# Norm of queries and keys on VectorE, middle butterfly on GpSimd, and issue order planned by phase

## The chip, the cores and the metric

One core of a Trainium2 chip. The metric is the device time of one launch in microseconds, median of the runs. One execution is also profiled; its trace gives the single durations. Engines are named as in the profile: PE (TensorE), PEld (its weight loads), DVE (VectorE), ACT (ScalarE), POOL (GpSimd), SP (SyncE, which issues the DMAs).

## What is computed

The input x is 128 x 32 x 256 (batch B, steps T, features N). Layer 0 integrates a coupled neuron model over the 32 steps (a fourth-order Runge-Kutta step per t) and sends each state through a feed-forward block with block-scaled quantization; the sum with x is the input of layer 1. Layer 1, on which the change lies, is an attention with normed queries and keys, 16 heads of 16, over the 32 tokens of each batch row, and then a feed-forward block with Hadamard rotation and ternary weights:

```
qkv = xn @ W_qkv
q = rms_norm(q, g_q);  k = rms_norm(k, g_k)          # over the 16 features of a head, eps 1e-6
attn = softmax(q k^T * 16 ** -0.5);  o = attn @ v
f = o + o @ W_out
gate, up = h_bitlinear(f, w_gate), h_bitlinear(f, w_up)
x = x + h_bitlinear(silu(gate) * up, w_down)

h_bitlinear(x, w) = act_quant(fwht(x)) @ weight_quant(w).T   # fwht: Walsh-Hadamard transform
```

## The kernel before

The kernel writes down all of its work as a list of items (`Work.add`): engine, a cost in us, a function that issues the instructions, the buffers read and written, and a rank. A buffer (`Buf`) is one of several slots of a pool (`wide`, `mid`, `slim`, `tiny` in SBUF; `ps_one`, four slots of one PSUM bank each, and `ps_two`, two slots of two banks, in the second phase). A planner then orders the list (`Work.order`, `Work.run`). `run` is a list scheduler over the five engines with costs, gaps between engines (`TAIL`, `HOP`, `WITHIN`), a shared port of DVE and POOL (`port=True`), slots that come free, and activation tables; run backward it gives priorities. `order` alternates the two 40 times and keeps the order with the earliest end, over both phases together. `emit` issues the items in that order, first all with a rank under 100 (phase one), then the rest (phase two). Engines take their instructions in the order of issue. `keep_warm` puts multiplications by zeros into long planned gaps of PE.

`fills=` adds an item to the writers of a buffer, so that later readers wait for it, but lets the item itself wait for nobody who wrote or read that buffer before.

Phase one (to about 430 us in the trace) has 32 steps: `step` (the integration, lines L552 to L653) and `ffn0` (layer 0's feed-forward block, L895 to L1017), and prepares the weights. Its last items per step write `xnT`, the normed and turned input of layer 1.

Phase two is `tokens(g)` for 32 groups g of 128 tokens each. Several groups are under way at a time. Per group:

- L1125, L1132: PE multiplies for queries and keys (`pqk`, 128 x 512) and for values (`pv`, columns 0 to 255 of a `ps_one` bank). L1141: ACT copies the values into `v_pad`. L1142: ACT squares `pqk` into `sq`.
- The norm: L1143, a DVE reduce over the 16 features of a head, gives 32 sums per token (`tiny`, 128 x 32). Function `rsqrt` (L1084 to L1111): POOL scales them (L1088), DVE makes a first estimate of the inverse root with integer arithmetic on the bits (L1091), and POOL improves it in ten operations (L1099 to L1109).
- L1148 and L1155: DVE multiplies queries and keys in `pqk` by it, into `qn` and `k_pad`; `pqk` is free then. L1160: POOL multiplies the queries by the gains `g_prod`, which also carry the constant `RSQRT**-2`.
- L1167, L1169: DVE transposes. L1177: logits on PE (32 x 32 tiles). L1192, L1196: DVE maximum and difference; L1199: ACT exponential; L1200: DVE transpose; L1207: PE, attention times values. L1218, L1221: DVE reciprocal and product. L526: PE transposes (a helper's line). L1230: PE, output and rotation.
- Quantization (L1071 reduce, L1078, L1079 scales; L1240; ACT L1246, L1250), a transposing DMA, L1263: gate and up, L1271: ACT silu, L1278: DVE product, into `it` (128 x 1024).
- The butterflies (L1294): three stages of the rotation, two additions of 128 x 512 each (sum and difference). In groups 0 to 28 the stages run on POOL, DVE, POOL; in 29 to 31 all on DVE.
- L526 turn, L1300 ACT copy, L1305 PE rotation by a 128 x 128 Hadamard matrix, quantization (L1071, L1310, L1313, L1317), a transposing DMA, L1328 down-projection, L1335 DVE sum, store.

L666, L671 and L678, small DVE operations of phase one in `mx_scales`, have an operand in PSUM.

Of the kernel before, what the change touches and what calls it, by code (L numbers as in the profile page):

```python
# [13 lines left out]
I32 = mybir.dt.int32  # L14
AF = mybir.ActivationFunctionType
ALU = mybir.AluOpType
AX = mybir.AxisListType
# [16 lines left out]
HEADS = 16  # L34
D_HEAD = 16
EPS_RMS = 1e-6
EPS_QUANT = 1e-5
RSQRT = 8.0 / 3.0

# [60 lines left out]
class Work:  # L100
# [81 lines left out]

    def run(self, forth):

# [9 lines left out]
        port, table = 0.0, None  # L194
        self.issued, self.last, self.gone = [], dict.fromkeys(ready), set()
        for item in self.items:
            item.open = len(item.after if forth else item.before)
            item.ready = 0.0
            for b in item.bufs:
                b.left, b.end = 0, 0.0  # L200
                if b.slots and not b.fixed:
                    b.slot = None
                for s in b.slots:
                    s.free = 0.0
        pools = {}
        for item in sorted(self.items, key=lambda i: i.prio):
            for b in item.bufs:
                if b.slots and b.slot is None and not b.left:
                    b.pool = pools.setdefault(id(b.slots), [])
                    b.pool.append(b)  # L210
                b.left += 1
        for item in self.items:
            if not item.open:
                ready[item.engine].append(item)
        done = []
        while len(done) < len(self.items):
            best = None
            for e, waiting in ready.items():
# [13 lines left out]
                if best is None or (t, item.prio) < (best[0], best[1].prio):  # L232
                    best = (t, item)
            assert best is not None, "every item waits for a slot"
            t, item = best
            ready[item.engine].remove(item)
            idle = item.engine == PE and t > now[PE] + 0.05
            item.start, item.end = t, t + item.cost + (self.COLD if idle else 0.0)
# [19 lines left out]
            for i in item.before if forth else item.after:  # L258
                i.ready = max(i.ready, item.end + (self.gap(item, i) if forth else self.gap(i, item)))
                i.open -= 1  # L260
                if not i.open:
                    ready[i.engine].append(i)
        return done

    def order(self):

        for item in self.items:
            for a in item.after:
                a.before.append(item)
            for b in item.bufs:  # L270
                b.fixed = b.slot is not None
            item.prio = item.rank
        best = math.inf
        for n in range(self.ROUNDS):
            self.strict = n > 0
            done = self.run(True)
            end = max(item.end for item in done)
            if end < best:
                best, chosen = end, done
                places = [(b, b.slot) for item in done for b in item.bufs]  # L280
                times = [(item, item.start, item.end) for item in done]
                ends = [(b, b.end) for item in done for b in item.bufs]
            for item in self.items:
                item.prio = -item.end
            self.strict = True
            self.run(False)
            for item in self.items:
                item.prio = -item.end
        for b, slot in places:
            b.slot = slot  # L290
        for b, end in ends:
            b.end = end
        for item, start, end in times:
            item.start, item.end = start, end
        self.keep_warm(chosen)
        return chosen
# [26 lines left out]
def kernel(  # L323
# [570 lines left out]
    def ffn0(t, q):  # L894
# [100 lines left out]

        add(POOL, 0.72, rsqrt, [], [ms], rank=rank)
        if t < T - LATE:
# [51 lines left out]
    for b_c, c_mat in zip(b_coup[:KPADS], coup):  # L1049
        k_pad = c_mat.rearrange("p c n -> p (c n)").rearrange("p (r a d) -> p r a d", a=4, d=D_HEAD)  # L1050
        pads_ready.append(
            add(POOL, 0.6, lambda k_pad=k_pad: nc.gpsimd.memset(k_pad, 0.0), [], [b_c], rank=float(T))
        )
        k_pads.append(Slot(k_pad))
# [8 lines left out]
    def heads(ap):  # L1063
        return ap.rearrange("p (h d) -> p h d", d=D_HEAD)
# [18 lines left out]

    def rsqrt(v, y, scale, eps, rank):  # L1084

        t, u = Buf(tiny), Buf(tiny)
        tt, ts = nc.gpsimd.tensor_tensor, nc.gpsimd.tensor_scalar
        add(POOL, 0.24, lambda: ts(v.ap, v.ap, scale, eps, MULT, ADD), [], [v], rank=rank)  # L1088
        add(
            DVE, 0.12,  # L1090
            lambda: nc.vector.tensor_scalar(  # L1091
                y.ap.bitcast(I32), v.ap.bitcast(I32), -0.5, float(0x5F3759DF), MULT, ADD
            ),
            [v], [y], rank=rank,
        )

        def steps():

            tt(t.ap, y.ap, y.ap, MULT)  # L1099
            tt(t.ap, t.ap, v.ap, MULT)  # L1100
            ts(t.ap, t.ap, -0.5, 1.5, MULT, ADD)
            tt(y.ap, y.ap, t.ap, MULT)

            tt(t.ap, y.ap, y.ap, MULT)
            tt(t.ap, t.ap, v.ap, MULT)
            ts(u.ap, t.ap, 1.0, -10.0 / 3.0, MULT, ADD)
            tt(u.ap, u.ap, t.ap, MULT)
            ts(u.ap, u.ap, 1.0, 5.0, MULT, ADD)
            tt(y.ap, y.ap, u.ap, MULT)  # L1109

        add(POOL, 2.4, steps, [v], [t, u, y], rank=rank, port=True)  # L1111

    def tokens(g):
# [25 lines left out]
        v_pad, sq, qn, k_pad = Buf(v_pads), Buf(mid), Buf(slim), Buf(k_pads)  # L1139
        sq_sum, rstd = Buf(tiny), Buf(tiny)  # L1140
        add(ACT, 0.26, lambda: nc.scalar.copy(v_pad.ap[:, :, :D_HEAD], heads(pv.ap[:, :N])), [pv], [v_pad], rank=rank)  # L1141
        add(ACT, 0.477, lambda: nc.scalar.activation(sq.ap, pqk.ap, AF.Square), [pqk], [sq], rank=rank)  # L1142
        add(DVE, 0.6, lambda: nc.vector.tensor_reduce(sq_sum.ap, heads(sq.ap), AX.X, ADD), [sq], [sq_sum], rank=rank)  # L1143

        rsqrt(sq_sum, rstd, 1.0 / D_HEAD, EPS_RMS, rank)
        add(
# [37 lines left out]
        for k in range(0, PAIRS, PAIRS // 2):  # L1184
            add(
                PE, 0.55, lambda k=k: logits(range(k, k + PAIRS // 2)), [qT, kT], fills=[pl], rank=rank,
                records=BT * PAIRS, small=True,
            )
# [23 lines left out]
        for k in range(0, HEADS, HEADS // 2):  # L1212
            add(
                PE, 0.63, lambda k=k: attend(range(k, k + HEADS // 2)), [exT, v_pad], fills=[po], rank=rank,
                records=BT * HEADS, small=True,
            )
# [67 lines left out]
        src = it  # L1284
        for s, engine in enumerate((POOL, DVE, POOL) if g < NT - 3 else (DVE, DVE, DVE)):
            dst = Buf(wide)
            for e, op in enumerate((ADD, SUB)):
# [7 lines left out]

                add(engine, 0.6 if engine == DVE else 1.228, butterfly, [src], fills=[dst], rank=rank, port=True)
            src = dst
# [119 lines left out]
```

## Time and profile before

| | us |
|---|---|
| runs of the kernel before | 867.62, 867.91, 868.57 (median 867.91) |
| the profiled execution's own time | 868.0 |
| its span in the trace, first to last instruction | 866.2 |
| busy in the span: PE, DVE, POOL, ACT | 795.1, 732.2, 615.9, 494.0 |
| butterflies L1294 on POOL: 116 of 1306 ns | 149.1 in all |
| butterflies L1294 on DVE: 76 of 727 ns | 53.3 in all |
| norm on POOL, L1088 and L1099 to L1109, 352 operations | 89.2 in all |
| L1091 on DVE: 32 of 321 ns | 10.3 in all |

A busy share is an average over stages with different limits, so the tables of stretches of the trace and the lists of waits are to be read by stage. The end of a PE instruction is modelled, since matmuls are pipelined. In a list of waits, a line names the waiting engine, its output and line, then the releaser, then the total in us, how many times, and the longest. In a timeline a line gives start, duration, engine, line, operation, output and inputs, and in brackets how long the engine had been idle and who released it. Durations of neighbours on DVE overlap, so that what one instruction costs its engine is the distance from start to start.

### The profile page before, as it was taken

To read this page: it belongs to the slowest core of one execution; us is meant where nothing else is said; L and a number is where in the kernel's file an instruction comes from. 1 tells how busy PE (TensorE), PEld (TensorE's weight loads), DVE (VectorE), ACT (ScalarE), POOL (GpSimd) and SP (SyncE) were. 2 spreads that over 40 slices of the span, in tenths; PEclk is the share of its full clock that TensorE was granted. 3 is DMA by queue.
4 is the path that set the end of the run, shared out by engine and by line. 5 is a ranking of instruction groups with operands and counts; after the bars stand their busy time and mean duration, and the time that the engine had idled before them with its cause. 6 is when DMAs were issued, how large, how long until landed. Compare 5 with 4: busy or idle time off the path is not lost. (4 is left out here: it accounts for less than half of the span.)

```text
span 866.2 us, 26286 instructions
## 1 busy us (share of the span) xinstructions
PE 795.1 (92%) x10506; PEld 598.6 (69%) x10506; DVE 732.2 (85%) x1863; ACT 494.0 (57%) x1009; POOL 615.9 (71%) x955
## 2 busy tenths in 40 slices
PE   7789999999999999997789999999999999899986
PEld 4566778877788788775456667666667676576765
DVE  6889989999989999998677887778878788887694
ACT  3233465655466665754335667666767555776755
POOL 5698898888768888899574776656685676676320
PEclk9999999999999999999799999999999999999999
DMA  7222232313122242435500113221221221221334
GB/s 241 84 38 53 59 82 59 74 49 83 35 65 68 70 134 56 92 67 110 117 2 15 27 39 65 49 49 32 52 50 48 56 48 42 48 43 46 60 68 86
DMA packets 128891, 55.53 MB, mean 64 GB/s; under 512 B 102144, under 2 KB 127616, under 8 KB 128768
## 3 DMA queue, kind: packets, MB, share of 16 engines
q1 hardware_dynamic: 128768, 53.85, 26.9%
q8 instruction: 82, 1.34, 0.6%
q14 instruction: 41, 0.34, 0.1%
HBM read 21.32 MB, written 8.39 MB: 34 GB/s over the span
## 5 line engine op out<-in xcount | busy, mean ns | idle before, releaser
L1294 POOL TENSOR_TENSOR wide<-wide 128x512 f32<-128x512 f32 x116 | 149.1, 1306 | 68.7 <-DVE wide L1278 33.6
L601 PEld LDWEIGHTS ps_stage<-slim,coup 128*128 128x128 f32 x1024 | 129.3, 192 | 18.1 <-ACT slim L594 10.6
L601 PE MATMUL ps_stage<-slim,coup 128*128 128x128 f32 x1024 | 139.4, 279 | 0.6 <-ACT slim L594 0.3
L608 POOL TENSOR_TENSOR slim<-slim,slim 128x256 f32<-128x256 f32 x96 | 72.4, 755 | 27.7 <-ACT slim L595 23.0
L587 PE MATMUL ps_stage<-slim,eye 128*128 128x256 f32 x256 | 76.6, 392 | 8.1 <-DVE slim L552 7.8
L587 PE MATMUL ps_stage<-drives,eye 128*128 128x256 f32 x256 | 79.2, 392 | 3.3 <-DVE ps_stage L552 2.0
L956 POOL TENSOR_TENSOR mid<-mid,tiny 128x512 f32<-128x512 f32 x64 | 66.2, 1047 | 3.7 <-DVE tiny L678 3.2
L964 POOL TENSOR_TENSOR wide_bf<-mid,tiny 128x512 bf16<-128x512 fp8e4 x64 | 66.5, 1050 | 1.4 <-DVE mid L888 1.1
L594 ACT ACTIVATE slim<-slim 128x256 f32<-128x256 f32 x96 | 39.3, 409 | 47.4 <-DVE slim L552 44.6
L1305 PE MATMUL ps_two<-had_ffn,wide 128*128 128x128 f32 x512 | 63.3, 278 | 1.3 <-DVE wide L1278 1.2
L595 ACT ACTIVATE slim<-slim 128x256 f32<-128x256 f32 x96 | 39.2, 408 | 43.1 <-DVE slim L552 43.0
L1305 PEld LDWEIGHTS ps_two<-had_ffn,wide 128*128 128x128 f32 x512 | 59.9, 192 | 5.4 <-ACT wide L1300 1.9
L1125 PE MATMUL ps_one<-w_qkv_sb,xnT 128*128 128x512 f32 x128 | 60.7, 599 | 0.5 <-DVE mid L1196 0.2
L1313 ACT ACTIVATE wide<-ps_two,magic,tiny 128x1024 f32<-128x1024 f32 x32 | 38.5, 1203 | 39.5 <-DVE tiny L1079 28.0
L587 PEld LDWEIGHTS ps_stage<-slim,eye 128*128 128x128 f32 x256 | 42.0, 190 | 24.0 <-DVE slim L552 16.1
L1294 DVE TENSOR_TENSOR wide<-wide 128x512 f32<-128x512 f32 x76 | 53.3, 727 | 5.9 <-POOL wide L1294 5.9
L1278 DVE SCALAR_TENSOR_TENSOR wide<-ps_two,tiny,mid 128x512 f32<-128x512 f32 x64 | 46.4, 737 | 12.0 <-ACT mid L1271 11.3
L1207 PEld LDWEIGHTS ps_one<-v_pad,mid 32*32 32x32 f32 x4096 | 42.2, 106 | 20.8 <-issue 15.4
L1271 ACT ACTIVATE mid<-ps_two,tiny 128x512 f32<-128x512 f32 x64 | 43.0, 686 | 21.9 <-PE ps_two L1263 21.6
L1207 PE MATMUL ps_one<-v_pad,mid 32*32 32x17 f32 x4096 | 48.0, 181 | 4.5 <-issue 3.0
L587 PEld LDWEIGHTS ps_stage<-drives,eye 128*128 128x128 f32 x256 | 40.3, 193 | 12.3 <-DVE ps_stage L552 7.7
L1263 PEld LDWEIGHTS <-slim_bf 128*128 128x128 bf16 x256 | 24.0, 97 | 34.3 <-issue 8.3
(169 smaller groups left out, 2188.7 us busy)
## 6 DMA issues: line engine op xcount, KB each, us to landing
x_step<-in_x_dram SPq DMA_DIRECT2D x32, 128.0 KB, 2.1
x_add<-in_x_dram SPq DMA_DIRECT2D x32, 128.0 KB, 2.1
x_dram<-slim SPq DMA_DIRECT2D x32, 128.0 KB, 1.9
slim<-x_dram SPq DMA_DIRECT2D x32, 128.0 KB, 2.6
out_dram<-slim SPq DMA_DIRECT2D x32, 128.0 KB, 1.7
raws<-in_L_ffn_w_gate_dram SPq DMA_DIRECT2D x4, 512.0 KB, 4.8
raws<-in_L_ffn_w_up_dram SPq DMA_DIRECT2D x4, 512.0 KB, 6.3
raws<-in_L_ffn_w_down_dram SPq DMA_DIRECT2D x4, 512.0 KB, 4.0
```

Source lines behind the costliest of these rows:

```text
L587: PE, cost, lambda: nc.tensor.matmul(ps[i].ap, lhsT=eyes[eye], rhs=src.ap, start=False, stop=False),
L594: add(ACT, 0.32, lambda: nc.scalar.activation(th.ap, qi.ap, AF.Tanh), [qi], [th], rank=rank, table="silu")
L601: nc.tensor.matmul(ps[i].ap[:, sl], lhsT=coup[i][:, c, sl], rhs=two(th.ap)[:, c, :], start=False, stop=(c == NC - 1 and m == NC - 1),)
L608: POOL, 0.685, lambda: nc.gpsimd.tensor_tensor(sq.ap, sq.ap, qi.ap, MULT),
L956: lambda it=it, ks=ks: nc.gpsimd.tensor_tensor(blocks(it.ap), blocks(it.ap), spread(binv.ap[:, ks], BLOCK), MULT),
L964: lambda b8=b8, ks=ks, sl=sl: nc.gpsimd.tensor_tensor(blocks(bq.ap[:, sl]), blocks(b8.ap), spread(bscl.ap[:, ks], BLOCK), MULT),
L1125: nc.tensor.matmul(pqk.ap, lhsT=xnT_flat[:, c, tok], rhs=w_qkv_sb[:, c, : 2 * N], start=(c == 0), stop=(c == NC - 1),)
L1207: nc.tensor.matmul(by_v(po.ap)[row, hd, :], lhsT=by_head(exT.ap)[row, hd, :], rhs=v_pad.ap[row, hd, :], start=True, stop=True,)
L1271: lambda pgu=pgu, act=act: nc.scalar.activation(act.ap, pgu.ap[:, :HALF], AF.Silu, scale=sgu.ap[:, 0:1]),
L1278: lambda pgu=pgu, act=act, sl=sl: stt(it.ap[:, sl], pgu.ap[:, HALF:], sgu.ap[:, 1:2], act.ap, MULT, MULT),
L1294: eng.tensor_tensor(dv[:, :, e, :], sv[:, :, 0, :], sv[:, :, 1, :], op)
L1305: nc.tensor.matmul(pfh.ap[:, sl], lhsT=iT.ap[:, sl], rhs=had_ffn, start=True, stop=True)
```

## The change

Three things are changed.

The norm: the sum over a head is written into the bank of `pv`, beside the values (columns 256 to 351, three pieces of 32). From there nine DVE operations, in one item with the reduce, scale it, make the estimate from the bits, and correct it by a cubic polynomial in the estimate's error. Each has an operand in PSUM. All of `rsqrt` on POOL is gone. The constant `RSQRT` is that of the polynomial.

The butterflies: groups 0 to 26 run all three stages on POOL; groups 27 to 31 run DVE, DVE, POOL.

The planner: `order` plans the phases one after the other, the second from where the first leaves engines and slots, each with 40 rounds (and two passes of new priorities in a round); dependencies across phases set only the earliest start. Some costs differ, and PE's restart cost is booked from a gap of 0.15 us on (0.05 before).

```diff
-RSQRT = 8.0 / 3.0
+RSQRT = 3.64945348
...
-    def run(self, forth):
+    def run(self, items, forth, before):
...
+            for a in item.after if forth else item.before:
+                if a in self.gone:
+                    item.ready = max(item.ready, a.end + self.gap(a, item))
+                elif (a.rank < self.SECOND) == (item.rank < self.SECOND):
+                    item.open += 1
...
+        if forth:
+            for item in before:
+                now[item.engine] = max(now[item.engine], item.end)
...
-            idle = item.engine == PE and t > now[PE] + 0.05
+            idle = item.engine == PE and t > now[PE] + 1.5 * self.COLD
...
-        best = math.inf
-        for n in range(self.ROUNDS):
-            self.strict = n > 0
-            done = self.run(True)
...
+        for second in (False, True):
+            items = [item for item in self.items if (item.rank >= self.SECOND) == second]
+            best = math.inf
+            for n in range(self.ROUNDS):
+                self.strict = n > 0
+                done = self.run(items, True, chosen)
...
+                for back in (True, False):
+                    for item in items:
+                        item.prio = -item.end
+                    if back:
+                        self.strict = True
+                        self.run(items, False, ())
...
-        add(POOL, 0.72, rsqrt, [], [ms], rank=rank)
+        add(POOL, 0.86, rsqrt, [], [ms], rank=rank)
...
-            add(POOL, 0.6, lambda k_pad=k_pad: nc.gpsimd.memset(k_pad, 0.0), [], [b_c], rank=float(T))
+            add(POOL, 1.0, lambda k_pad=k_pad: nc.gpsimd.memset(k_pad, 0.0), [], [b_c], rank=float(T))
...
-    def rsqrt(v, y, scale, eps, rank):
...
+    POLY = (-1.14571778, 1.36854794, -1.82472059, RSQRT)
+
+    def norms(sq, y, place, scale, eps, rank):
...
+        n = 2 * HEADS
+        x, e, t = Buf(tiny), Buf(tiny), Buf(tiny)
+        ts = nc.vector.tensor_scalar
 
         def steps():
...
+            v, g, u = (place.ap[:, N + k * n : N + (k + 1) * n] for k in range(3))
+            nc.vector.tensor_reduce(v, heads(sq.ap), AX.X, ADD)
+            ts(x.ap, v, scale, eps, MULT, ADD)
+            ts(g.bitcast(I32), x.ap.bitcast(I32), -0.5, float(0x5F3759DF), MULT, ADD)
+            nc.vector.tensor_tensor(t.ap, g, x.ap, MULT)
+            nc.vector.tensor_tensor(u, g, t.ap, MULT)
+            ts(e.ap, u, -1.0, None, ADD)
+            stt(u, u, POLY[0] - 1.0, e.ap, ADD, MULT)
+            stt(u, u, POLY[1], e.ap, ADD, MULT)
+            stt(t.ap, u, POLY[2], e.ap, ADD, MULT)
+            stt(y.ap, t.ap, POLY[3], g, ADD, MULT)
+
+        add(DVE, 1.55, steps, [sq], [x, e, t, y], fills=[place], rank=rank)
...
-        add(DVE, 0.6, lambda: nc.vector.tensor_reduce(sq_sum.ap, heads(sq.ap), AX.X, ADD), [sq], [sq_sum], rank=rank)
-
-        rsqrt(sq_sum, rstd, 1.0 / D_HEAD, EPS_RMS, rank)
+        norms(sq, rstd, pv, 1.0 / D_HEAD, EPS_RMS, rank)
...
-                PE, 0.55, lambda k=k: logits(range(k, k + PAIRS // 2)), [qT, kT], fills=[pl], rank=rank,
+                PE, 0.48, lambda k=k: logits(range(k, k + PAIRS // 2)), [qT, kT], fills=[pl], rank=rank,
...
-                PE, 0.63, lambda k=k: attend(range(k, k + HEADS // 2)), [exT, v_pad], fills=[po], rank=rank,
+                PE, 0.57, lambda k=k: attend(range(k, k + HEADS // 2)), [exT, v_pad], fills=[po], rank=rank,
...
-        for s, engine in enumerate((POOL, DVE, POOL) if g < NT - 3 else (DVE, DVE, DVE)):
+        for s, engine in enumerate((POOL, POOL, POOL) if g < NT - 5 else (DVE, DVE, POOL)):
...
-                add(engine, 0.6 if engine == DVE else 1.228, butterfly, [src], fills=[dst], rank=rank, port=True)
+                add(engine, 0.6 if engine == DVE else 1.25, butterfly, [src], fills=[dst], rank=rank, port=True)
```

More of the change, by code (lines that the diff above doesn't have):

```diff
@@ L194, in run @@
         port, table = 0.0, None
-        self.issued, self.last, self.gone = [], dict.fromkeys(ready), set()
-        for item in self.items:
-            item.open = len(item.after if forth else item.before)
+        self.issued, self.last, self.gone = [], dict.fromkeys(ready), set(before)
+        for item in items:
+            item.open = 0
             item.ready = 0.0
+            for a in item.after if forth else item.before:
[3 more added lines that the diff above has]
+                    item.open += 1
             for b in item.bufs:
@@ L204, in run @@
                     s.free = 0.0
+        if forth:
+            for item in before:
+                now[item.engine] = max(now[item.engine], item.end)
+                self.last[item.engine] = item
+                table = item.table or table
+                for b in item.bufs:
+                    for s in b.slots:
+                        s.free = 0.0
+            for item in before:
+                for b in item.bufs:
+                    if b.slots:
+                        s = b.slots[b.slot]
+                        s.free = max(s.free, item.end + item.tail + self.TAIL[item.engine] + 0.06)
         pools = {}
-        for item in sorted(self.items, key=lambda i: i.prio):
+        for item in sorted(items, key=lambda i: i.prio):
             for b in item.bufs:
@@ L211, in run @@
                 b.left += 1
-        for item in self.items:
+        for item in items:
             if not item.open:
@@ L215, in run @@
         done = []
-        while len(done) < len(self.items):
+        while len(done) < len(items):
             best = None
@@ L258, in run @@
             for i in item.before if forth else item.after:
[L259 to L262, printed above, removed]
+                if (i.rank < self.SECOND) == (item.rank < self.SECOND):
+                    i.ready = max(i.ready, item.end + (self.gap(item, i) if forth else self.gap(i, item)))
+                    i.open -= 1
+                    if not i.open:
+                        ready[i.engine].append(i)
         return done
@@ L272, in order @@
             item.prio = item.rank
-        best = math.inf
-        for n in range(self.ROUNDS):
-            self.strict = n > 0
-            done = self.run(True)
[L277 to L294, printed above, removed]
+        chosen = []
+        for second in (False, True):
[4 more added lines that the diff above has]
+                done = self.run(items, True, chosen)
+                end = max(item.end for item in done)
+                if end < best:
+                    best, order = end, done
+                    places = [(b, b.slot, b.end) for item in done for b in item.bufs]
+                    times = [(item, item.start, item.end) for item in done]
+                for back in (True, False):
+                    for item in items:
+                        item.prio = -item.end
+                    if back:
+                        self.strict = True
+                        self.run(items, False, ())
+            for b, slot, end in places:
+                b.slot, b.end = slot, end
+            for item, start, end in times:
+                item.start, item.end = start, end
+            chosen += order
         self.keep_warm(chosen)
@@ L1082, in quantum @@
         return am, sc
-    def rsqrt(v, y, scale, eps, rank):
[L1086 to L1095, printed above, removed]
-        def steps():
[L1099 to L1111, printed above, removed]
+    POLY = (-1.14571778, 1.36854794, -1.82472059, RSQRT)
[3 more added lines that the diff above has]
+        ts = nc.vector.tensor_scalar
+        def steps():
+            v, g, u = (place.ap[:, N + k * n : N + (k + 1) * n] for k in range(3))
[10 more added lines that the diff above has]
+        add(DVE, 1.55, steps, [sq], [x, e, t, y], fills=[place], rank=rank)
     def tokens(g):
@@ L1139, in tokens @@
         v_pad, sq, qn, k_pad = Buf(v_pads), Buf(mid), Buf(slim), Buf(k_pads)
-        sq_sum, rstd = Buf(tiny), Buf(tiny)
+        rstd = Buf(tiny)
         add(ACT, 0.26, lambda: nc.scalar.copy(v_pad.ap[:, :, :D_HEAD], heads(pv.ap[:, :N])), [pv], [v_pad], rank=rank)
         add(ACT, 0.477, lambda: nc.scalar.activation(sq.ap, pqk.ap, AF.Square), [pqk], [sq], rank=rank)
-        add(DVE, 0.6, lambda: nc.vector.tensor_reduce(sq_sum.ap, heads(sq.ap), AX.X, ADD), [sq], [sq_sum], rank=rank)
-        rsqrt(sq_sum, rstd, 1.0 / D_HEAD, EPS_RMS, rank)
+        norms(sq, rstd, pv, 1.0 / D_HEAD, EPS_RMS, rank)
         add(
```

## The prediction

> **What bounds the kernel now.** I read the table of stretches first, because the change lies almost wholly in the second phase (from about 430 us). Columns: stretch, its length, busy us of PE (instructions), PEld, DVE, ACT, POOL, then granted clock, DMA share, GB/s.
>
> ```profile
> 430.00:440.00 10.00, 8.91 (x30) 4.85 (x31) 3.87 (x9) 3.12 (x6) 3.98 (x15) 1.00 0.14 27
> ...
> 600.00:650.00 50.00, 46.27 (x981) 34.53 (x981) 39.74 (x96) 34.28 (x48) 35.08 (x64) 0.97 0.22 49
> 650.00:700.00 50.00, 46.23 (x1045) 35.32 (x1044) 40.85 (x97) 31.03 (x45) 32.12 (x52) 1.00 0.20 48
> ...
> 820.00:840.00 20.00, 17.75 (x121) 12.34 (x120) 18.30 (x39) 13.47 (x19) 5.47 (x4) 1.00 0.41 86
> ```
>
> In the seven stretches from 450 to 800 us the busy times sum to PE 324.6 of 350, DVE 283.1, POOL 234.8, ACT 223.5. PE is closest to full and idles 25.4 us; DVE has 67 us of holes. L1125 runs 108 times there, four per group, so 27 groups pass, one per 13.0 us.
>
> Next, who waits in that stretch: DVE's waits, then PE's (total us, times, longest).
>
> ```profile
> DVE slim L1148 <- POOL tiny L1109: 16.4, 16, 2.7
> ...
> DVE coup L1155 <- POOL tiny L1109: 7.3, 7, 1.6
> DVE wide L1294 <- POOL wide L1294: 5.9, 6, 1.8
> ...
> DVE tiny L1091 <- POOL tiny L1088: 1.7, 5, 0.4
> ```
>
> ```profile
> PE ps_one L526 <- DVE slim L1221: 2.6, 4, 0.9
> PE ps_two L1263 <- ACT wide L1313: 2.6, 3, 1.5
> PE ps_two L1263 <- DMA slim_bf<-slim_bf: 2.0, 3, 1.1
> PE ps_two L526 <- DVE wide L1278: 2.0, 3, 1.0
> ```
>
> DVE stands 31.3 us behind POOL, nearly all behind exactly what the change takes away. PE's own waits are small and scattered: by releaser over the whole list 10.4 us DVE, 5.4 ACT, 1.7 POOL, 3.3 DMA, 3.7 issue. So a late DVE reaches PE at several places, none of them the norm itself. One norm by the timeline (start, us):
>
> ```profile
> 602.91 0.22 POOL L1088 TENSOR_SCALAR tiny<-tiny 128x32 f32<-128x32 f32 x1 [1.94 <-DVE tiny L1143]
> 604.12 0.24 POOL L1099 TENSOR_TENSOR tiny<-tiny 128x32 f32<-128x32 f32 x1 [1.00 <-DVE tiny L1091]
> ...
> 607.35 0.25 POOL L1109 TENSOR_TENSOR tiny<-tiny,tiny 128x32 f32<-128x32 f32 x1
> ```
>
> ```profile
> 607.64 0.42 DVE L1148 TENSOR_TENSOR slim<-ps_one,tiny 128x256 f32<-128x256 f32 x1 [2.07 <-POOL tiny L1109]
> ```
>
> The reduce began at 602.17, so the norm took 5.5 us from reduce to multiplication, four changes of engine included.
>
> **What the Trainium skill says.** SBUF — State Buffer, Who interferes with whom: a two-port DVE instruction, or one with two SBUF inputs, and GpSimd exclude each other. The trace agrees: L1091, SBUF to SBUF, takes 115 ns at least and 1262 at most (mean 321); L666 and L678, with an operand in PSUM, 186 and 182 at the same 128x32. VectorE: DVE Perf Modes, The DRAIN you can't avoid: a read on DVE of what DVE just wrote still needs a semaphore. The timeline shows what that costs, starts of three small operations:
>
> ```profile
> 414.01 0.19 DVE L666 TENSOR_SCALAR ps_sum<-tiny 128x32 f32<-128x32 f32 x1
> 414.24 0.19 DVE L678 TENSOR_SCALAR tiny<-ps_sum 128x32 int32<-128x32 int32 x1
> 414.34 0.18 DVE L671 TENSOR_SCALAR tiny<-ps_sum 128x32 int32<-128x32 int32 x1
> ```
>
> Dependent 0.23, independent 0.10. Perfetto Trace Analysis, Optimizing Scalar/DVE Operations, gives about 125 ns of access cost per PSUM operation; the 0.10 here is below that, so I use the trace. PSUM — Partial Sum Buffer, PSUM bank collisions: different engines must be kept apart by bank, even at disjoint columns. In before every PSUM tile passes between engines by listed dependencies, so no row there prices a clash.
>
> **The change part by part**, for the 27 groups between 450 and 800 us unless said.
>
> Norm off POOL. Eleven small operations go: 89.2 us over 32 groups, 2.8 each, and ten gaps of 0.08, so 3.6 us of POOL per group; and L1091 from DVE (0.32 less 0.07 of overlap: 0.25). Nine dependent DVE operations come. Bounds: 0.10 each if none waits for its forerunner (0.9 us), 0.23 if all do (2.1). I take 0.21 (1.9): each reads the one before, and L785 starts 0.19 behind L781, whose result it reads (417.98 and 417.79). The small three-operand form has no row, and at 128x512 it costs 737 against 680 for the two-operand one. The planner books 1.55 for reduce and nine; I expect 0.6 + 1.9 = 2.5. What queues behind it on DVE is any group's next evacuation.
>
> Middle butterfly to POOL. Two DVE additions go, 0.60 from start to start each: 1.2 us. POOL gets two at 1.27: 2.5. POOL's sum is -3.6 + 2.5 = -1.1 us per group, at 67% busy; no new bound. The three stages now run on one engine: six times 1.27 = 7.6 us, against 2.5 + 1.2 + 2.5 = 6.2 plus hand-offs (18.3 us of POOL waits for DVE there, 5.9 of the reverse). This costs nothing while other groups keep PE supplied; uncovered, it is 1.4 us a group.
>
> Sum for DVE: busy 283.1 + 27 x (-1.2 - 0.25 + 1.9) = 295.3, no waits for POOL. Before: 283.1 + 31.3 = 314.4. Relief 19.1 us. It reaches PE only through the waits put down to DVE, ACT and POOL, 17.5 us. I take half: **-8.7 us**; bounds 0 (PE's order and PSUM set the pace) and -17.5. With 0.10 per operation DVE gains another 27 us.
>
> Place in the bank of v. The nine operations write the bank into which L1132 multiplies and from which L1141 copies, and the planner's list has no dependency between them. A v matmul or copy issued during the norm must wait for its end. Before, the matmul stands anywhere: 580.63 with the reduce at 582.52, or 628.19 with it at 623.68. By chance 2.5 of 13 us: 5 of 27 groups, each waiting half the norm, 1.3: 6.5 us on PE, half of it made up since delayed work is ready: **+3**. The same on ACT (64% busy) I cost at nothing; its idle time covers it, uncovered 6.5. Bounds 0 and 13. Against it, the bank of q and k comes free some 3 us sooner and that of v later.
>
> Ramp. The first reduce starts at 433.91, its L1148 at 438.37. With 2.5 us, 436.4: **-2.0**; bounds -3 and 0.
>
> Drain. Groups 29 to 31 move six additions to POOL, 27 and 28 bring four to DVE and take four off POOL. DVE is full from 829 to 849, where six at 0.6 are 3.6; a POOL pair is 2.5 against 1.2 in the last chain, +1.3, and the four add up to 1.3: **-1.0**; bounds -3 and +2.
>
> Order and costs. All DMAs stay the same work, but each queue, SP's too, gets a new order. The corrected costs are close to rows (1.25 for a median of 1.27; 0.86 for 0.25 + 0.59 and a gap; 1.0 for 0.89), and the planner's allowance for an idle PE only alters paper times. Phase one's work is unchanged; PE is 98% busy from 100 to 350, and its tail to 430 hangs on POOL and DVE. The joint order of before could mix the phases on paper while they are emitted one after the other; planning them apart can only move a few waits there, in either direction. **0**, bounds -4 and +4. The new polynomial constant only alters a factor: 0.
>
> Sum: -8.7 + 3 - 2.0 - 1.0 = -8.7. The profiled execution took 868.0 (span 866.2 and 1.8 around it); 868.0 - 8.7 = **859.3**. The median, 867.91, is 0.1 away.
>
> **Rivals.**
> A. *The relief is used wholly*: -17.5 in place of -8.7, no bank waits, -2 and -1: 847.5. For it: 67 us of DVE holes. Against: DVE at 295 of 350 is still the second fullest, and PE's waits are scattered.
> B. *PE goes on as it does*: only ramp and drain remain: 865. For it: PE is 93% busy, 0.2 us of PE's waits name POOL's norm. Against: 10.4 us of waits behind DVE.
> C. *The bank of v becomes the bound*, slower than before. Without bank waits the sum is -11.7; at 1.3 us of PE each it is eaten up from nine stalled groups of 32. With every second group: 16 x 1.3 = 20.8, 868.0 - 11.7 + 20.8 = 877. For it: v does not depend on the norm in the list, and the planner books the norm a microsecond short. Against: often the matmul lies microseconds away.
> D. *The norm does not leave the path*, since a busy DVE delays it as POOL did; then B's time.
>
> **Numbers.** Forecast (850 to 864) 0.44; A (838 to 850) 0.12; B and D (864 to 868) 0.16; C and any worse order (868 to 885) 0.28. About 0.2%, 1.7 us, is what a measurement tells from no change. Below 866.2: 0.44 + 0.12 + 0.08 = 0.64; within: 0.08 + 0.02 = 0.10; above: 0.26. The range 846 to 876 leaves out some 0.08 below and 0.11 above.
>
> **What will show it.** Right: the nine small DVE rows start 0.2 apart; DVE's waits for POOL fall from 31 to near 5 us; PE idles 17 to 21 us between 450 and 800. Wrong: v_pad or the v matmul waits long for a tiny DVE operation (C); DVE's holes move to other releasers with PE idle the same (B); phase one's end moves by over 4 us.

## The result, and the profile after

The changed kernel takes 907.54 us (four runs, 904.48 to 912.02) against 867.76 us of the kernel before beside it: a ratio of 1.0462, 95% interval 1.0417 to 1.0507, so some 40 us slower where 8.7 us faster was forecast. The profiled execution took 907.63, its span is 905.8 us, and its mean granted clock is 0.967 (0.986 before). In the changed kernel L1123 is the reduce, L1124 to L1132 are the nine operations of the norm, L1155 is the v matmul, L1164 the copy into `v_pad`, L1169 the multiplication of the queries, L1315 the butterflies, L1299 the product before them.

The loss lies in the second phase. The first qk matmul starts at 429.1 us (431.3 before), and from there to the end of the span it is 476.7 us against 434.9. The stretches of after, with the columns that the prediction explains:

```profile
430.00:450.00 20.00, 14.54 (x100) 8.55 (x99) 12.96 (x43) 3.55 (x8) 2.17 (x3) 0.76 0.00 1
450.00:800.00 350.00, 309.62 (x6502) 224.79 (x6500) 269.24 (x797) 201.10 (x294) 196.24 (x170) 0.97 0.19 41
600.00:650.00 50.00, 43.24 (x957) 32.72 (x946) 36.79 (x105) 31.02 (x44) 29.76 (x27) 1.00 0.22 40
650.00:700.00 50.00, 46.45 (x960) 33.59 (x959) 37.24 (x107) 28.85 (x42) 33.18 (x29) 0.93 0.17 41
```

and two of the same stretches of before:

```profile
430.00:450.00 20.00, 16.70 (x235) 9.52 (x235) 11.62 (x25) 6.86 (x12) 11.75 (x44) 1.00 0.07 14
450.00:800.00 350.00, 324.62 (x7020) 236.55 (x7012) 283.10 (x684) 223.50 (x321) 234.84 (x446) 0.99 0.20 44
```

Between 450 and 800 us PE now idles 40.4 of 350 us (25.4 before), and every other engine has become emptier too, DVE included: 80.8 us of holes in place of 66.9. No engine has become full. Something makes all of them wait.

DVE's waits in that stretch (engine, output and line, releaser, total us, times, longest) name POOL nowhere any more:

```profile
DVE tiny L1094 <- PE ps_one L1251: 14.3, 9, 3.9
DVE ps_one L1123 <- ACT mid L1165: 13.0, 10, 3.3
DVE wide L1299 <- ACT mid L1292: 12.1, 11, 3.1
```

The 31.3 us that DVE stood behind POOL are gone, as the prediction had it. PE's list shows what came instead, and so does ACT's:

```profile
PE ps_one L1155 <- DVE tiny L1132: 22.6, 14, 3.2
PE ps_one L1251 <- ACT slim L1246: 3.1, 2, 2.7
PE ps_one L1155 <- DVE tiny L1101: 2.5, 1, 2.5
```

```profile
ACT v_pad L1164 <- PE ps_one L1155: 29.8, 11, 7.4
...
ACT v_pad L1164 <- DVE tiny L1132: 17.3, 7, 3.4
```

L1132 is the last of the nine small operations. The v matmul reads nothing that it writes; the two write different columns of one `ps_one` tile, which is one PSUM bank, and the wait goes when the norm has another slot (e9, below). Whether the bank or the tile is what counts, no run here separates. 14 times in this stretch PE stands in front of it, 1.6 us each on the mean, 22.6 us in all; a fifteenth wait, 2.5 us put down to L1101, ends with a norm as well (the matmul starts 2.89 us behind its reduce). In the whole of before, the largest sum that the v matmul waited for any releaser was 1.2 us. ACT's copy stands behind the same operation for another 17.3 us, and behind the late matmul for 29.8 (11.7 in the whole of before, and nothing behind the norm).

A timeline of DVE shows one norm (start, duration, engine, line):

```profile
433.41 0.69 DVE L1123 TENSOR_REDUCE ps_one<-mid 128x32 f32<-128x512 f32 x1 [6.93 <-ACT mid L1165]
434.14 0.19 DVE L1124 TENSOR_SCALAR tiny<-ps_one 128x32 f32<-128x32 f32 x1
434.36 0.20 DVE L1125 TENSOR_SCALAR ps_one<-tiny 128x32 int32<-128x32 int32 x1
...
435.97 0.19 DVE L1132 SCALAR_TENSOR_TENSOR tiny<-tiny,ps_one 128x32 f32<-128x32 f32 x1
436.26 0.42 DVE L1169 TENSOR_TENSOR slim<-ps_one,tiny 128x256 f32<-128x256 f32 x1
```

The nine start 0.23 us apart, and from the reduce to L1169 it is 2.85 us (4.46 before, 433.91 to 438.37). The norm by itself is faster. Now PE in a stretch that such a norm reaches:

```profile
458.25 0.61 PE L1375 MATMUL ps_two<-zeros 128*128 128x256 bf16 x4
462.03 2.04 PE L1155 MATMUL ps_one<-w_qkv_sb,xnT 128*128 128x256 f32 x4 [3.17 <-DVE tiny L1132]
...
464.43 1.05 PE L1228 MATMUL ps_one<-v_pad,mid 32*32 32x17 f32 x64
...
466.29 1.75 PE L1251 MATMUL ps_one<-w_oh,slim 128*128 128x256 f32 x4
```

The reduce ahead of it starts at 459.15 and that norm ends 2.8 us later; at that moment the v matmul starts, 3.17 us after PE's last work. Its four instructions then take 2.04 us, where they take 1.10 to 1.13 after most other stalls, and the attention of another group behind it takes 1.05 us for 64 instructions where it took 0.73 just before the stall. Such a stall is paid twice: the clock granted from 462 to 470 us is 0.65. The Trainium skill (TensorE: Matmul & The Clock Gate, Part 1) says that the gate halves the clock of an idle array and gives it back after activity; this stretch agrees, from 1.13 to 2.04 us for the same four instructions. The length of a stall does not settle by itself whether this happens: of the 15 stalled v matmuls three took 2.04 or 2.05 us, behind stalls of 3.17, 2.48 and 2.54 us, while those behind 2.57 us (at 636.59) and 2.69 us (at 786.49) took 1.13 and 1.10. Over the whole span PE is busy 811.5 us, 16.4 more than before. Some 6 of these are more multiplications by zeros (`keep_warm`; by lines 39.5 us in 243 instructions, 33.2 in 206 before); the other 10300 instructions are the same number, and take some 10 us longer.

**By chance, or not.** The start of a v matmul against the nearest reduce, from the timelines of PE and DVE: in after, 15 of the 27 norms between 450 and 800 us are followed by a v matmul within 2.5 to 3.3 us of their start, which is the moment they end, and 8 more start 0.9 to 1.5 us behind the start of a v matmul, which is the moment that ends. In 23 of 27 groups the two stand edge to edge. In before, 2 of 27 are at the first distance and none at the second.

### The profile page after: what moved, and what is told of

Read it like the earlier page. It is cut to its first block, busy times and chain, and to the rows that moved or that the text cites. A ratio compares the mean times of both kernels' runs of the same rounds, so it can differ in the third digit from the quotient of the medians.

```text
span 905.8 us, 26297 instructions
## 1 busy us (share of the span) xinstructions
PE 811.5 (90%) x10543; PEld 610.6 (67%) x10543; DVE 747.0 (82%) x2063; ACT 484.8 (54%) x1003; POOL 596.0 (66%) x659
## 4 chain that ended last, share of the span: by engine, by line
PE 23%; DVE 19%; ACT 6%; issue 3%; DMA 1%; DVEq 0%; ACTq 0%; SPq 0%
PE ps_two L1326 3%; PE ps_one L1148 3%; PE ps_one L1155 3%; PE ps_two L1284 3%; PE ps_two L549 2%; DVE ps_one L1123 2%; DVE tiny L1094 2%; PE ps_one L1251 2%; PE ps_one L1228 2%; PE ps_one L1198 2%; DVE wide L1315 1%; ACT wide L1334 1%; DVE wide L1299 1%; PE ps_one L1349 1%; DVE mid L1221 1%
## 5 line engine op out<-in xcount | busy, mean ns | idle before, releaser
L1315 POOL TENSOR_TENSOR wide<-wide 128x512 f32<-128x512 f32 x172 | 215.9, 1283 | 95.9 <-DVE wide L1299 49.7
L1181 POOL TENSOR_TENSOR slim<-slim,g_prod 128x256 f32<-128x256 f32 x32 | 23.3, 728 | 124.9 <-DVE slim L1169 102.5
L610 PE MATMUL ps_stage<-drives,eye 128*128 128x256 f32 x256 | 81.1, 400 | 2.4 <-DVE ps_stage L575 1.8
L987 POOL TENSOR_TENSOR wide_bf<-mid,tiny 128x512 bf16<-128x512 fp8e4 x64 | 68.4, 1077 | 2.0 <-DVE mid L911 1.9
L1326 PEld LDWEIGHTS ps_two<-had_ffn,wide 128*128 128x128 f32 x512 | 61.8, 196 | 8.8 <-ACT wide L1321 6.2
L617 ACT ACTIVATE slim<-slim 128x256 f32<-128x256 f32 x96 | 39.3, 410 | 52.4 <-DVE slim L575 51.3
L1148 PE MATMUL ps_one<-w_qkv_sb,xnT 128*128 128x512 f32 x128 | 62.9, 617 | 2.9 <-ACT v_pad L1164 1.5
L1155 PE MATMUL ps_one<-w_qkv_sb,xnT 128*128 128x256 f32 x128 | 39.1, 436 | 29.1 <-DVE tiny L1132 26.2
L1299 DVE SCALAR_TENSOR_TENSOR wide<-ps_two,tiny,mid 128x512 f32<-128x512 f32 x64 | 46.2, 738 | 16.6 <-ACT mid L1292 16.3
L1334 ACT ACTIVATE wide<-ps_two,magic,tiny 128x1024 f32<-128x1024 f32 x32 | 38.5, 1202 | 37.2 <-DVE tiny L1102 24.2
L1292 ACT ACTIVATE mid<-ps_two,tiny 128x512 f32<-128x512 f32 x64 | 42.6, 685 | 25.8 <-PE ps_two L1284 25.2
L1094 DVE TENSOR_REDUCE tiny<-ps_two 128x1 f32<-128x1024 f32 x32 | 38.8, 1212 | 21.1 <-PE ps_two L1326 20.9
L1155 PEld LDWEIGHTS ps_one<-w_qkv_sb,xnT 128*128 128x128 f32 x128 | 24.9, 211 | 39.1 <-issue 17.5
```

The lines of the kernel that those rows point to most:

```text
L610: PE, cost, lambda: nc.tensor.matmul(ps[i].ap, lhsT=eyes[eye], rhs=src.ap, start=False, stop=False),
L987: lambda b8=b8, ks=ks, sl=sl: nc.gpsimd.tensor_tensor(blocks(bq.ap[:, sl]), blocks(b8.ap), spread(bscl.ap[:, ks], BLOCK), MULT),
L1094: lambda: nc.vector.tensor_reduce(am.ap[:, 0:1], src.ap[:, :n], AX.X, ALU.max, apply_absolute_value=True),
L1148: nc.tensor.matmul(pqk.ap, lhsT=xnT_flat[:, c, tok], rhs=w_qkv_sb[:, c, : 2 * N], start=(c == 0), stop=(c == NC - 1),)
L1155: nc.tensor.matmul(pv.ap[:, :N], lhsT=xnT_flat[:, c, tok], rhs=w_qkv_sb[:, c, 2 * N :], start=(c == 0), stop=(c == NC - 1),)
L1299: lambda pgu=pgu, act=act, sl=sl: stt(it.ap[:, sl], pgu.ap[:, HALF:], sgu.ap[:, 1:2], act.ap, MULT, MULT),
```

## The theories and the experiments

Theory "bank": nearly the whole loss comes of the nine operations sharing the bank of `pv` without the planner knowing that this excludes the v matmul and the copy. Its first rival, "booking": the norm is booked at 1.55 us and takes 2.85, so the order is made for a DVE that is less full than it is. A second, "load": nine operations are too much for DVE, or six additions for POOL, wherever they are put. The third, "order": the planner by phase makes a worse order. The expectations put these in their own words; where one numbers its theories, "bank" is the first. Ratios are to the kernel before, with the 95% interval.

**The three parts alone.** e8 is the kernel before with the planner and the costs of the change, e7 with its butterflies, e6 with its norm; e1 is the changed kernel with the norm of before.

```diff
# e7, on the kernel before
-        for s, engine in enumerate((POOL, DVE, POOL) if g < NT - 3 else (DVE, DVE, DVE)):
+        for s, engine in enumerate((POOL, POOL, POOL) if g < NT - 5 else (DVE, DVE, POOL)):
# e1, on the changed kernel (RSQRT = 8 / 3 and rsqrt() as before)
-        norms(sq, rstd, pv, 1.0 / D_HEAD, EPS_RMS, rank)
+        add(DVE, 0.6, lambda: nc.vector.tensor_reduce(sq_sum.ap, heads(sq.ap), AX.X, ADD), [sq], [sq_sum], rank=rank)
+        rsqrt(sq_sum, rstd, 1.0 / D_HEAD, EPS_RMS, rank)
```

e1. 

> The changed kernel with the norm of before (reduce on DVE, eleven small operations on POOL, L1091 on DVE), everything else of the change kept: the three butterfly stages on POOL and the order planned by phase. Theory 1 (the bank of v: PE's v matmul waits for the norm, 29 us of PE idle in the trace of after, and ACT's copy waits 23 more): the 40 us go away with the new norm, 860 to 870 us. Theory 2 (the planner books the norm a microsecond short, so DVE is late everywhere): also 860 to 870, since the old norm is not booked short by more than before. Theory 3 (the butterflies on POOL or the order by phase cost the time): stays at 890 to 907.

e6. 

> The kernel before with the new norm alone (booked 1.55, bank not declared): butterflies and planner as before. Theory 1 and 2 both put the loss into the norm: 895 to 915, with 15 to 30 us of PE waiting at the v matmul for the norm. If the loss needs the planner by phase or the butterflies on POOL beside it: 865 to 880.

e7. 

> The kernel before with the butterflies alone moved (three stages on POOL in groups 0 to 26, DVE, DVE, POOL after that; costs as before). With the old norm POOL then has 8.3 + 2.5 us of some 13 per group, still no bound, and DVE loses 1.2: 855 to 866. If POOL becomes the bound through the old norm's long chain: 870 to 885.

e8. 

> The kernel before with the planner and the costs of the change alone (order by phase, logits 0.48, attention 0.57, rsqrt of phase one 0.86, memset 1.0, the idle allowance): norm and butterflies as before. With the kernel that has planner and butterflies at 857.2, the gain of 11 us belongs to one of them: planner 857 to 862 if it is the order, 864 to 870 if it is the butterflies.

| kernel | us | ratio | PE busy of 350 us |
|---|---|---|---|
| e1, change without its norm | 857.15 | 0.9865 (0.9835 to 0.9895) | 331.9 |
| e6, norm alone | 924.58 | 1.0632 (1.059 to 1.0673) | 300.1 |
| e7, butterflies alone | 878.94 | 1.0095 (1.0077 to 1.0114) | 319.2 |
| e8, planner and costs alone | 864.43 | 0.9933 (0.9916 to 0.995) | 330.9 |

The loss is the norm's: alone it costs more than in the whole change, and without it the change gains 1.4%. "Order" falls with e8. Three numbers were missed: e1 is faster than expected, e6 slower, and e7, taken for a gain, is a loss. In e6 PE shows the same wait in the same place (L1130 is the v matmul there, L1107 the last operation of the norm):

```profile
PE ps_one L1130 <- DVE tiny L1107: 20.8, 10, 3.3
```

**The booking and the bank told.** e2 books the norm at what it takes; e5 tells the planner of the bank (booked at 1.60), e3 does both.

```diff
-        add(DVE, 1.55, steps, [sq], [x, e, t, y], fills=[place], rank=rank)
+        add(DVE, 2.65, steps, [sq], [x, e, t, y], fills=[place], rank=rank)   # e2
+        add(DVE, 2.65, steps, [sq], [x, e, t, y, place], rank=rank)          # e3
+        add(DVE, 1.6, steps, [sq], [x, e, t, y, place], rank=rank)           # e5
```

e2. 

> The changed kernel with one number altered: the planner books 2.65 us for the norm item instead of 1.55, which is what the trace of after shows from the reduce's start to the last operation's end. Theory 1 (bank of v): the planner still knows no dependency between the norm and the v matmul, so PE goes on waiting for the norm, 20 to 30 us in the trace, and the time stays at 895 to 910. Theory 2 (booked short): it falls to 865 to 880.

e3. 

> As the kernel with 2.65 us booked, and the norm item also declares the bank of v as written, so that the planner puts it behind the v matmul and ACT's copy of v. Nothing that is computed changes. Theory 1 (bank of v): the waits of PE's v matmul for the norm vanish (under 2 us in the trace) and the time falls to 855 to 875. Theory 2 (booked short): no better than the kernel with the cost alone. Theory 3 (butterflies, order by phase): stays over 890.

e5. 

> The changed kernel with the bank of v declared as written by the norm item, and the item booked at 1.60 us, so nearly as short as in the change (1.55). It completes the square of the two causes: 907.5 with neither mended, 886.8 with the cost alone, 869.6 with both. If the two add (20.7 and 17.3 us), 888 to 892. If the undeclared bank is the main cause and the booking matters only because it puts v inside the norm (theory 1), 866 to 878. If the booking alone is the cause (theory 2), 898 to 908.

Measured: e2 886.83 (1.0216, 1.0176 to 1.0257), e5 880.36 (1.0110, 1.009 to 1.013), e3 869.56 (1.0006, 0.9988 to 1.0023). In e2 the wait is still there, shorter per time:

```profile
PE ps_one L1155 <- DVE tiny L1132: 17.8, 14, 2.7
```

In e5 and e3 it is gone. The booking takes a good half of the loss, the bank told (and booked at 1.60) three quarters, both together all of it. e2 falls between what "bank" and "booking" had expected. The two parts don't add up (2.5% and 3.5%, together 4.6%), and each edit changes the whole order, so these three don't say by themselves how much is the bank's.

**Another place for the three pieces.** e4 puts them into SBUF tiles; e9 gives them a `ps_one` slot of their own and leaves everything else, the short booking too, as in the change; e10 is e9 with the booking of e2.

```diff
# e4
+        own = [Buf(tiny) for _ in range(3)]
-            v, g, u = (place.ap[:, N + k * n : N + (k + 1) * n] for k in range(3))
+            v, g, u = (b.ap for b in own)
# e9; e10 has 2.65 in place of 1.55 besides
-        norms(sq, rstd, pv, 1.0 / D_HEAD, EPS_RMS, rank)
+        norms(sq, rstd, Buf(ps_one), 1.0 / D_HEAD, EPS_RMS, rank)
```

e4. 

> The changed kernel with the three PSUM pieces of the norm put into SBUF tiles of 128x32 instead (booked 1.55 as in the change), so that the norm shares no bank with v but all nine operations may be held up by POOL's butterflies. Theory 1 (bank of v): PE's v matmul no longer waits for the norm; the nine operations last longer than 0.23 us each where POOL is at work (mean 0.3 to 0.5), and the time is 865 to 885. Theory 2 (booked short): the norm is booked even shorter of what it takes, so 900 to 920.

Measured: 924.27, 1.0638 (1.0607 to 1.0668). The v matmul no longer waits for the norm, as "bank" says, but the number is missed by far, since five of the nine operations have become slower (mean ns of one in the third place, groups of instructions by line):

```profile
L1126 DVE TENSOR_SCALAR tiny<-tiny 128x32 int32<-128x32 int32 x32 | 15.3, 479 | 1.1
L1127 DVE TENSOR_TENSOR tiny<-tiny,tiny 128x32 f32<-128x32 f32 x32 | 15.9, 498 | 1.1
...
L1130 DVE SCALAR_TENSOR_TENSOR tiny<-tiny,tiny 128x32 f32<-128x32 f32 x32 | 6.2, 192 | 1.1
```

Each of the nine took 186 to 199 ns in after. The Trainium skill (SBUF — State Buffer, Who interferes with whom) says that a DVE instruction in a two-port mode, or with two SBUF inputs, and GpSimd hold each other up at the port they share. The timelines agree: of the 160 operations of the five slowed lines 54 began while POOL was at work, and took 0.69 to 1.18 us on the mean of a line; the other 106 took 0.18 to 0.19. The four scalar_tensor_tensor operations took 192 ns, but none of the 128 began while POOL was at work, so they don't show that this form escapes. One norm, POOL and then DVE:

```profile
495.18 7.37 POOL L1316 TENSOR_TENSOR wide<-wide 128x512 f32<-128x512 f32 x6
```

```profile
501.41 1.18 DVE L1129 TENSOR_SCALAR tiny<-tiny 128x32 f32<-128x32 f32 x1
502.62 0.19 DVE L1130 SCALAR_TENSOR_TENSOR tiny<-tiny,tiny 128x32 f32<-128x32 f32 x1
```

POOL's six additions are over before the first scalar_tensor_tensor starts. The place in PSUM serves a purpose, then, and e4 mixes the bank with a longer norm: it decides nothing between the theories.

e9. 

> The changed kernel with one thing altered: the three pieces of the norm lie in a ps_one slot of their own, taken for the norm item alone, and no longer in the bank of v. Operands stay in PSUM, the item stays booked at 1.55. It costs the planner one more of four slots for some 2.5 us per group. Theory 1 (bank of v): the v matmul's wait for the norm is gone, and with it the part of the loss that the booking does not explain; near the kernel with the bank told and booked short (ratio 1.011): 870 to 885. Theory 2 (booked short only): stays at 895 to 910.

e10. 

> As the kernel with the norm's own slot, but booked at 2.65 us. Neither cause is left, so near the kernel with the bank told and 2.65 booked (ratio 1.0006): 860 to 872. If there is a third cause in the nine DVE operations themselves (DVE full), no better than 875.

Measured: e9 871.83 (20 runs), 1.0031 (1.0018 to 1.0045); e10 867.43, 0.9982 (0.9959 to 1.0006). In e9 nothing is edited but the slot (the planner's order follows from it), and what is left of PE's wait at the v matmul between 450 and 800 us is

```profile
PE ps_one L1155 <- DVE tiny L1132: 1.5, 1, 1.5
```

Only 3 of its 29 norms there are followed at their end by a v matmul (15 of 27 in after). The ratio goes from 1.0462 to 1.0031, so with the short booking the shared bank costs 37 us of the 40 (4.3 of 4.6 points); with 2.65 booked, e2 against e10, it costs 2.3 points. Both carry the point or so by which orders differ (below).

Between the spans of after and e9 lie 905.8 - 870.8 = 35.0 us. PE's busy time falls from 811.5 to 796.3, 15.2 of them, and its idle time from 94.3 to 74.5, 19.8 of them: more than half is standing still. Of the 15.2, some 6 are fewer multiplications by zeros (33.7 us by lines, 39.5 in after); the rest, some 9, is the same 10300 instructions taking less time, at a clock of 0.985 against 0.967.

"Booking" by itself, with the bank no longer shared with v, is e9 against e10, half a per cent. A part of PE's waiting for the norm has only moved in e9: in the same stretch other matmuls wait 12.2 us for it, the largest sum being

```profile
PE ps_one L1251 <- DVE tiny L1132: 4.3, 4, 2.0
```

In e5, booked short too, PE waits 12.1 us for the norm at such lines, in e10 and e3, with 2.65 booked, 0.7 and 3.1. This fits a slot that the norm holds longer than the planner counts on. The larger effect of the booking in e2 presumably comes of moving the v matmul and the copy against the norm. "Load" falls with e10 and e3: the nine operations and the six additions are all there, and the loss is not.

**Who is held.** e13 makes the norm follow the v matmul in the planner's list, and leaves the copy on ACT free to meet it.

```diff
-        add(DVE, 1.55, steps, [sq], [x, e, t, y], fills=[place], rank=rank)
+        add(DVE, 1.55, steps, [sq], [x, e, t, y], fills=[place], rank=rank, after=[v_item])
```

> The changed kernel with one dependency added for the planner: the norm item comes after the v matmul of its group (not after ACT's copy of v); booked at 1.55, bank shared as in the change. PE then never waits for the norm, but ACT's copy still can. If PE's stalls are the loss (22.6 us seen in 350): 870 to 882, with PE's waits at v under 2 us. If ACT's copy, held by the norm 7 times in the stretch with all that queues behind it, is as costly: 885 to 900.

Measured: 898.41, 1.0343 (1.0303 to 1.0383), PE busy 312.1 of 350. PE's waits for the norm at L1155 are gone, and ACT has taken them over:

```profile
ACT v_pad L1164 <- DVE tiny L1132: 34.2, 14, 4.0
```

From after to e13 just over a point of the 4.6 is won back, no more than orders differ by. So a hold of ACT on the same bank seems nearly as dear as one of PE. Why is argued: behind the copy stands every other step of ACT in its order, silu, quantization and square, and PE waits for those in turn. It fits that PE's waits put down to ACT in this stretch are 12.4 us, against 6.7 in after and 2.4 in e10.

**How much is the order's luck.** Every edit that alters a cost alters most of the order (in e11 fewer than a tenth of DVE's operations of phase two stand in the place that they have in before). Three kernels change only the booked cost of a POOL butterfly by 0.002 to 0.005 us: before (e11), after (e12), e1 (e15).

```diff
-                add(engine, 0.6 if engine == DVE else 1.25, butterfly, [src], fills=[dst], rank=rank, port=True)
+                add(engine, 0.6 if engine == DVE else 1.252, butterfly, [src], fills=[dst], rank=rank, port=True)
```

(This is e12; 1.23 for 1.228 in e11, 1.255 for 1.25 in e15.)

e11. 

> The kernel before with the planner's cost of a butterfly on POOL at 1.230 instead of 1.228: no instruction is added or removed, only the order may come out another. It measures how far the time moves with the order alone. If the order is settled by the real limits: within 0.3% of before. If the list scheduler's outcome is largely chance: up to 1.5% either way, and differences between kernels below that say little.

e12. 

> The changed kernel with the planner's cost of a butterfly on POOL at 1.252 instead of 1.250: only the order may come out another. If the loss is by the norm's hidden waits and booking, whatever the order, 890 to 925. If the order of the changed kernel was merely an unlucky one: 860 to 885.

e15. 

> The kernel with the old norm, planner and butterflies of the change (ratio 0.9865), the planner's cost of a butterfly on POOL at 1.255 instead of 1.250, so that only the order may change. If the gain is the order by phase with the butterflies: 0.983 to 0.991. If it was one lucky order: 0.995 to 1.005.

Measured: e11 868.93, 0.9998 (0.9981 to 1.0014); e12 909.1, 1.0475 (1.0426 to 1.0523); e15 865.94, 0.9967 (0.9945 to 0.9988), a point above e1's 0.9865. An order is worth up to 1% in these three pairs. The 4.6% are no accident of one order, and in e12 PE waits 38.3 us at the v matmul for the norm between 450 and 800 us; but e1's own gain, e7's loss and the difference of e9 and e10 are within what orders differ.

**What DVE's time is worth.** e14 is the own slot with four operations of the norm less. It leaves the correcting polynomial out, and the operation that is left hands on `u`, the mean square times the squared estimate, in place of the inverse root, so that queries and keys are not normed. The own slot and the booking, 1.73 in place of 2.65, are not shown.

```diff
-            ts(e.ap, u, -1.0, None, ADD)
-            stt(u, u, POLY[0] - 1.0, e.ap, ADD, MULT)
-            stt(u, u, POLY[1], e.ap, ADD, MULT)
-            stt(t.ap, u, POLY[2], e.ap, ADD, MULT)
-            stt(y.ap, t.ap, POLY[3], g, ADD, MULT)
+            ts(y.ap, u, 1.0, None, MULT)
```

> The kernel with the norm's own slot and right booking, with four of the nine small operations left out (the correcting polynomial; the inverse root is then not corrected, so part of the computation is missing) and booked 0.92 us less. Four operations of 0.23 us in 32 groups are 29 us less of DVE. If DVE's fill is what keeps this version above the old norm: about half of it comes out at the end, 0.982 to 0.990 of before. If PE's order sets the pace: 0.995 to 1.000.

Measured: 854.13, 0.9818 (0.9793 to 0.9842), 1.6 points under e10, about 14 us. The four are 32 x 4 x 0.23 = 29 us of DVE. So about half of DVE's time comes out at the end; with the point (9 us) that orders differ by, anything from a fifth to four fifths.

**The best version.** e16 is e1 with POOL's part of the old norm booked at 3.25 in place of 2.4.

```diff
-        add(POOL, 2.4, steps, [v], [t, u, y], rank=rank, port=True)
+        add(POOL, 3.25, steps, [v], [t, u, y], rank=rank, port=True)
```

> The kernel with the old norm, planner and butterflies of the change, its ten operations on POOL booked at 3.25 us (what the trace shows from first to last) instead of 2.4. If right booking helps where it also marks what else waits: 0.978 to 0.985 of before. If booking matters only with a hidden dependency beside it, as the new norm's own slot suggests (1.003 to 0.998): 0.984 to 0.990.

Measured: 854.17 (851.62 to 855.35), 0.9817 (0.979 to 0.9845), the fastest of the kernels that compute everything: the planner and the butterflies of the change with the norm of before. That this booking is the cause rather than a good order is not shown.

## Why the prediction was wrong

**The step that failed is "Place in the bank of v".** It named the mechanism and the place, and rival C priced one hit at 1.3 us, close to the 1.6 measured. What was mis-sized is how often, and whom else it holds.

- *How often.* The step took the v matmul to "stand anywhere", so 2.5 of 13 us, 5 of 27 groups. Measured: 14 of 27 stall PE, and 23 of 27 stand edge to edge. In e9, where the two share no bank, a v matmul starts during a norm or at its end in 5 of 29 groups; by chance would have been about right there. Why they meet in the changed kernel is argued, not shown: the norm and the v matmul are both allowed to be first in a slot of `ps_one`, so the moment at which a slot comes free makes both ready, and the order sends both off at once.
- *Half made up.* The step took half of each wait to be made up. Hardly any was: in the whole run PE waits 26.2 us for the norm, against 0.7 in e10, and PE's idle time is 94.3 us against 68.5. That is 25.5 us more waiting and 25.8 us more idling, as a balance of two orders. The remaining 11.4 of the 37.2 us between the two spans are PE's busy time, 811.5 against 800.1, with as much time in multiplications by zeros (39.5 and 39.3): the same work at a lower clock (0.967 against 0.983), a term that the step did not have.
- *ACT at nothing.* The step let ACT's idle time cover its hold. e13 leaves that hold and takes PE's away, and still stands at 1.0343, with 12.4 us of PE's waits put down to ACT between 450 and 800 us. In after itself they are 6.7 against 5.4 in before, so there the direct part is small. Idle time of ACT covered little there, since what waited was on the way to PE.
- *Its bounds* of 0 and 13 were therefore far too near; rival C ended at 877 for every second group. The 907 need almost three times as many stalls, nothing made up, and the lower clock; and none of the relief that the sum had counted on.

**The relief of DVE was not on the path.** The forecast was -8.7 of 19.1 us. The sum for DVE was right: it expected +0.45 us of busy time per group, and DVE's whole busy time rose from 732.2 to 747.0, 0.46 a group. The waits for POOL went to nothing, too (31.3 us; the list of before has 0.6 more, behind L1160). But with the bank out of the way e10 stands at 0.9982 (0.9959 to 1.0006) and e9 at 1.0031, where the sum without bank waits was -11.7 us (0.9865). And e1, whose DVE stands behind POOL's norm more often than in before (its L1173 is L1148 of before, L1134 the norm's last line), has 0.9865 (0.9967 in the order of e15):

```profile
DVE slim L1173 <- POOL tiny L1134: 25.1, 24, 2.2
...
DVE tiny L1116 <- POOL tiny L1113: 8.1, 11, 2.3
```

Rival B's view of this part, PE "goes on as it does", was the better one. Why is argued, not shown: DVE's waits for POOL may have lain in holes that another group's lateness would have made anyway, and what the removal saved in waiting may have gone into the work that it added, since by e14 work on DVE does reach the end in part.

**Norm off POOL**: right in the main. Nine at 0.23 (0.21 taken), three-operand form no dearer, reduce to L1169 2.85 (2.5 taken).

**Middle butterfly to POOL**: not settled. -1.2 us of DVE, +2.5 of POOL as counted, and no cost on PE forecast. Under the old planner it costs 0.95% (e7), where the norm stays on POOL and DVE's wait for it grows from 16.4 to 29.0 us; under the new one e1 is 0.7% under e8. Both are within what orders differ by.

**Ramp**: the gain lost. The first L1169 comes at 436.26, as forecast (436.4), which is in part luck: the reduce began 0.50 us sooner (433.41) and what follows took 2.85 us for 2.5. From 430 to 450 us PE is busy 14.54 us, not 16.70, at a clock of 0.76; v matmuls wait for norms there twice (1.36 us at 436.21, 2.29 at 445.45).

**Order at 0**: missed, and outside its bounds of -4 and +4: e8 gives 0.67% or -5.8 us, in which one order's luck may have its part. Phase one ended 2.2 us sooner in after.

**Drain**: not measured by itself.

## What to carry to other kernels

Scratch space in a bank that another engine fills was a dependency here, though the columns were apart: it must be in the list that the order is made from, or have a slot of its own, since an order made without it may bring the two together in most groups rather than by chance. Before a wait of a busy engine is booked as a gain, ask what the waiting work would have waited for next; here the end of 31 us of waits shows no gain (e10, 0.9982). A stall of PE is to be priced with the slower matmuls behind it, here four to five tenths as much again (11.4 us on 25.8 beside e10, some 9 on 19.8 beside e9).

## What was not expected of the hardware

Small DVE operations of 128 x 32 took 186 to 199 ns, two operands or three, as long as one of them lay in PSUM, and with all of them in SBUF 0.18 to 0.19 us while POOL stood still, but 0.69 to 1.18 us where POOL was at work at their start (e4). PE's clock goes with its idle time, by and large: busy 298 of 350 us at a clock of 0.93 (e4), 300 at 0.95 (e6), 310 at 0.97 (after), 319 at 0.99 (e9), 335 at 1.00 (e14).
